# Two semaphore waits on TensorE for each block's gathers in a graph attention kernel

## The chip, the cores and the metric

The kernel runs on one core of a Trainium2 chip. The metric is the device time of one execution in microseconds (us). The engines of the core have their own instruction queues: TensorE (PE in the profile, its weight loads PEld), VectorE (DVE), ScalarE (ACT), GpSimd (POOL) and SyncE (SP), which here only issues DMAs.

## What is computed

One layer of attention over the edges of a graph with 12,500 nodes of 128 features (8 heads of 16) and 212,500 edges, sorted by their target node `dst`:

```
h = relu(layernorm(x))
q, v = h @ Wq.T + bq, h @ Wv.T + bv            # per node
k = edge_attr @ Wk.T + bk                      # per edge
in_m, out_m, diag_m = sum(q[src]*k), sum(q[dst]*k), sum(q[src]*q[dst])   # per edge and head
score = (softmax over each dst of in_m + of out_m + of diag_m) * edge_weight**lam
out = x + leaky_relu(segment_sum(score * v[dst]) @ Wo.T + bo, 0.1)
```

The three softmaxes are each taken over the edges of one target node.

## The kernel before

All of the work is in `ordered_path`; a second path, `general_path`, is in the program for other inputs and does not run.

**Preparation** (to about 178 us in the profile). Node features are loaded and normalized, q is computed and written to a table in device memory (`q_table`), once more as three bf16 terms (`q3_table`). Indices of the edges are brought into shape. On the way, the first gathers and edge loads are issued.

**The edge loop** (line 1091) is written out in full. Edges come in blocks of 512 (`BE`), 4 to a partition (`JN`). The 416 blocks are cut into S = 5 streams; turn g = 5t + s works on block t of stream s, and there are 420 turns. For each turn:

- `gather` (L604): four indirect DMAs on POOL (L608) fetch the rows q[src] into a tile `qq`. They are issued LOOK = 9 turns ahead; `qq` has QQ = 11 buffers, so the gathers of block b wait until DVE has read block b - 11.
- `fetch_edges` (L593): SP loads the edge features, 6 turns ahead.
- `turn` (L937): PE transposes the edge features, ACT copies them out of PSUM (L942).
- `project` (L946): PE makes k: one matmul for the bias (L948) and four f32 matmuls, 8 instructions in the profile (L950). `k_ps` has two PSUM buffers, so k of block g waits for DVE's multiply of block g - 2.
- `spread_q` (L955): PE multiplies the one-hot rows `oh` by a window of the q table (L959) to get q[dst], since targets are sorted; ACT copies it to `qq` (L961). ACT makes the one-hots from the relative targets in two operations (L934, L935, `one_hots`).
- `logits` (L963): DVE multiplies q[src] by q[dst] (L968), both by k (L969), and sums over each head (L971).

Every fifth turn the logits of five blocks are transposed and scanned on DVE along the edges: a running maximum (L1001, L1004), then running sums of the exponentials (L1025, L1029). The sums at the ends of segments are picked by a one-hot matrix (`select`, L1038; PE, L1062) and written to device memory.

**The last part** (from about 2300 us) divides the sums, multiplies by v, applies Wo and writes the output.

The order of each engine's instructions is the order in which the program calls them: `pin` (L575) ties each instruction to the one before it on its engine, by an order without a semaphore, and keeps the name of the last one in `pinned[engine]`. In turn g the calls come in this order: `gather(g + 9)`, `fetch_edges(g + 6)`, `project(g + 1)`, `turn(g + 2)`, `spread_q(g + 2)`, `logits(g)`, `one_hots`, and then the work of the scans, which differs with s. So k of block g is made by PE at the start of turn g - 1.

Blocks 0 to 8 are gathered in the preparation code (L868), the others in the loop; POOL has nothing else to do in the loop.

Of the kernel before, what the change touches and what calls it, by code (L numbers as in the profile page):

```python
# [472 lines left out]
def ordered_path(ctx: ExitStack, tc: tile.TileContext, flag, x, src, dst, edge_attr, edge_weight,  # L473
# [17 lines left out]
    nc = tc.nc  # L491
# [76 lines left out]
    LOOK, QQ, AHEAD, EA = 9, 11, 6, 7  # L568
# [4 lines left out]
    pinned = {}  # L573

    def pin(inst):  # L575

        engine = str(inst.ins.engine)
        if engine in pinned:
            tc.add_manual_dep(inst.ins, pinned[engine], mybir.DependencyInfo(
                mybir.DependencyClass.NoSync, mybir.DependencyReason.DATA), reason="in order")  # L580
        pinned[engine] = inst.ins.name
        return inst
# [5 lines left out]
        q.dma_start(to[cut:RW - 1, :], t[cut * RC:top].rearrange("(r c) -> r c", c=RC))  # L588
        q.dma_start(to[RW - 1:RW, :E - top], t[None, top:E])

    qqs, st, eas = {}, {}, {}

    def fetch_edges(g):  # L593
        if g < S * T:
            ea = load.tile([P, JN * F], F32, name="ea", bufs=EA)
            b0 = (g % S * G + g // S) * BE
            n = min(BE, E - b0)
            if n < BE:
                nc.vector.memset(ea, 0.0)
            pin(nc.sync.dma_start(ea[:n // JN, :],  # L600
                                  edge_attr[b0:b0 + n, :].rearrange("(p j) f -> p (j f)", j=JN)))
            eas[g] = ea

    def gather(g):  # L604
        if g < S * T:
            qq = gath.tile([P, JN, 2, F], F32, name="qq")
            for j in range(JN):
                pin(nc.gpsimd.indirect_dma_start(  # L608
                    out=qq[:, j, 0, :], out_offset=None, in_=q_table,
                    in_offset=bass.IndirectOffsetOnAxis(  # L610
                        ap=src_i[:, g % S * G + g // S, j:j + 1], axis=0)))
            qqs[g] = qq

    def units(t, lo, n, c):
# [13 lines left out]
    with tc.tile_pool(name="prep", bufs=1) as prep, \  # L628
# [239 lines left out]
        for g in range(LOOK):  # L868
            gather(g)
# [30 lines left out]
    with tc.tile_pool(name="work", bufs=2) as work, \  # L900
# [5 lines left out]
        def block_rows(t):  # L906
            lo = t if t < G else t - 1
            return lo, slice(0, S * G) if t < G else slice(1, S * G + 1)

        def fetch(t):  # L910

            if t >= T:
                return
            at, part = block_rows(t)
            relb = load.tile([K3, S, BE], BF, name="relb")
            pin(nc.sync.dma_start(relb, rel_d[part].rearrange("(s b) e -> s b e", b=G)
                                  [None, :, at, :].to_broadcast([K3, S, BE])))
            fa = load.tile([4 * S, BE], BF, name="fa", bufs=4)
            for s in range(S):
                pin(nc.sync.dma_start(fa[4 * s:4 * s + 4], fa_d[s * G + t]))  # L920
            _, base_v[t] = nc.values_load_multi_w_load_instructions(
                bases[0:1, t, 0:S], engines=[mybir.EngineType.SP], min_val=0, max_val=N - 1,
                skip_runtime_bounds_check_because="the indices of nodes are below N")
            win = load.tile([K3, S, F], BF, name="win")
            for s in range(S):
                pin(nc.sync.dma_start(win[:, s, :], q3_table[bass.ds(base_v[t][s] * 3, K3), :]))
            st[t] = dict(relb=relb, fa=fa, win=win)

        def one_hots(t, s):

            if s == 0:
                st[t]["oh"] = work.tile([K3, S, BE], BF, name="oh")
            d = st[t]["relb"][:, s, :]
            pin(nc.scalar.activation(d, d, AF.Abs, bias=before[:K3]))  # L934
            pin(nc.scalar.activation(st[t]["oh"][:, s, :], d, AF.Relu, bias=1.0, scale=-1.0))  # L935

        def turn(g):  # L937
            eT_ps = ps.tile([P, JN, P], F32, name="eT_ps", bufs=2)
            for j in range(JN):
                pin(nc.tensor.transpose(eT_ps[:, j, :], eas[g][:, j * F:(j + 1) * F], ident))  # L940
            eT = work.tile([P, JN, P], F32, name="eT", bufs=3)
            pin(nc.scalar.copy(eT, eT_ps))  # L942
            eTs[g] = eT
            del eas[g]

        def project(g):  # L946
            k_ps = ps.tile([P, JN, F], F32, name="k_ps", bufs=2)
            pin(nc.tensor.matmul(k_ps, ones3, bk3, start=True, stop=False))  # L948
            for j in range(JN):
                pin(nc.tensor.matmul(k_ps[:, j, :], eTs[g][:, j, :], wk, start=False,  # L950
                                     stop=(j == JN - 1)))
            ks[g] = k_ps
            del eTs[g]

        def spread_q(g):  # L955
            s, d = g % S, st[g // S]
            qd_ps = ps.tile([P, JN, F], F32, name="qd_ps")
            for j in range(JN):
                pin(nc.tensor.matmul(qd_ps[:, j, :], d["oh"][:, s, j * P:(j + 1) * P],  # L959
                                     d["win"][:, s, :], start=(j == 0), stop=(j == JN - 1)))  # L960
            pin(nc.scalar.copy(qqs[g][:, :, 1, :], qd_ps))  # L961

        def logits(g):  # L963
            s, t = g % S, g // S
            if s == 0:
                lTs[t] = scan.tile([P, JN, S, H3], F32, name="lT")
            prod = work.tile([P, JN, 3, F], F32, name="prod")
            pin(nc.vector.tensor_mul(prod[:, :, 2, :], qqs[g][:, :, 0, :], qqs[g][:, :, 1, :]))  # L968
            pin(nc.vector.tensor_mul(prod[:, :, 0:2, :], qqs[g],  # L969
                                     ks[g][:, :, None, :].to_broadcast([P, JN, 2, F])))  # L970
            pin(nc.vector.tensor_reduce(lTs[t][:, :, s, :],  # L971
                                        prod.rearrange("p j i (h d) -> p j (i h) d", d=DIM), AX.X,
                                        ALU.add))
            del ks[g], qqs[g]
# [103 lines left out]
        def later(f, t):  # L1078
            if 0 <= t < T:
                f(t)  # L1080

        fetch(0)
        fetch(1)
        for s in range(S):
# [6 lines left out]
        for g in range(end + 2 * S):  # L1091
            s, t = g % S, g // S
            if g < end:
                gather(g + LOOK)
                fetch_edges(g + AHEAD)
            if g + 1 < end:
                project(g + 1)
            if g + 2 < end:
                turn(g + 2)
                spread_q(g + 2)  # L1100
            if g < end:
                logits(g)
            if t + 1 < T:
                one_hots(t + 1, s)
            if s == 0:
                later(turn_logits, t - 1)
                later(turn_sums, t - 2)
            elif s == 1:
                later(scan_max, t - 1)
            elif s == 2:  # L1110
                later(to_rows, t - 2)
                later(powers, t - 1)
            elif s == 3:
                later(scan_sums, t - 1)
                if t + 2 < T:
                    fetch(t + 2)
            else:
                later(select, t - 1)
                later(put_rows, t - 2)

    edges.close()

# [64 lines left out]
@with_exitstack  # L1187
def kernel(ctx: ExitStack, tc: tile.TileContext, x, src, dst, edge_attr,
                              edge_weight, Wq, bq, Wk, bk, Wv, bv, Wo, bo, lam, out):

    nc = tc.nc
    given = (x, src, dst, edge_attr, edge_weight, Wq, bq, Wk, bk, Wv, bv, Wo, bo, lam, out)
    flags = ctx.enter_context(tc.tile_pool(name="flags", bufs=1))
    flag = flags.tile([1, 1], I32, name="flag")
    ordered_path(tc, flag, *given)
    other = nc.values_load(flag[0:1, 0:1], min_val=0, max_val=1)
    with tc.If(other != 0):
        general_path(tc, *given)  # L1200
# [29 lines left out]
```

## Time and profile before

| what | value |
|---|---|
| median of 4 runs | 2479.02 us (2473.14 to 2480.8) |
| profiled execution | 2478.28 us |
| its span in the trace | 2476.5 us |
| granted TensorE clock, mean | 0.806 |
| PE, DVE, ACT, POOL busy in the span | 71%, 86%, 61%, 68% |
| first and last gather of the run (L608) start | 100.4 us, 2293.9 us |
| L608: count, mean | 1680, 989 ns |
| L968, L969, L971: count and mean | 420 each; 683, 1214, 1753 ns |

Busy time is the time in which an engine executes; waits, and what it takes to issue an instruction, are not in it. In the groups of the page, a line ends with the idle time of the engine just ahead of these instructions and with what ended most of it; "issue" means that the profile shows nothing that it waited for. In the timeline each row has its start, its duration, the engine, the line, the operation, and in brackets the idle time before it and its releaser. The chain of work that ended last is followed back from the last instruction of the run. The windows give each engine's busy time and, in brackets, its number of instructions in a stretch of time, then the granted TensorE clock, the share of the DMA engines and the GB/s.

### The profile page before, as it was taken

How to read it: one execution, taken by the hardware profiler on the slowest of the kernel's cores; microseconds unless marked ns; L12 is line 12 of the kernel's file. 1: busy time of each engine (PE TensorE's matmuls, PEld its weight loads, DVE VectorE, ACT ScalarE, POOL GpSimd, SP SyncE). 2: the span in 40 equal slices, each digit the busy share in tenths (PEclk: the TensorE clock that was granted, in tenths of full speed). 3: DMA queues.
4: the chain of work that ended last, by engine and by line, in shares of the span. 5: the costliest groups of instructions: out<-in, count | busy, mean ns of one | idle time of the engine just before them, and what ended most of it. 6: DMA issues, size and time to landing. Idle time of an engine off the chain costs nothing.

```text
span 2476.5 us, 35097 instructions
## 1 busy us (share of the span) xinstructions
PE 1748.3 (71%) x10635; PEld 1411.6 (57%) x10635; DVE 2139.5 (86%) x2178; ACT 1499.1 (61%) x2806; POOL 1694.2 (68%) x1714
## 2 busy tenths in 40 slices
PE   5327777777677777777777777776777777767476
PEld 4215666665565565556556566565565666656355
DVE  6559999999989899898999989988899988999463
ACT  5547766766566556665656666566565665656354
POOL 2557777777777777777777777777777777777000
PEclk9658888878887778887878878788787787788599
DMA  7755455554444544445444444444444445443532
GB/s 223 241 171 158 142 150 143 143 150 129 136 137 131 148 127 137 138 136 144 128 136 136 143 138 128 137 137 136 141 130 136 136 130 150 129 136 88 118 101 76
DMA packets 307123, 345.21 MB, mean 139 GB/s; under 512 B 134531, under 2 KB 225944, under 8 KB 306613
## 3 DMA queue, kind: packets, MB, share of 16 engines
q1 hardware_dynamic: 252474, 229.91, 30.7%
q0 software_dynamic: 54448, 112.96, 17.8%
q8 instruction: 85, 1.39, 0.2%
q14 instruction: 116, 0.95, 0.1%
HBM read 309.91 MB, written 32.76 MB: 138 GB/s over the span
## 4 chain that ended last, share of the span: by engine, by line
DVE 24%; DMA 23%; issue 18%; POOL 13%; PE 12%; ACT 9%; SPq 0%; DVEq 0%; ACTq 0%; POOLq 0%
DMA qq<-q_table,src_i 20%; POOL qq L608 13%; DVE prod L969 8%; DVE prod L968 6%; PE k_ps L950 4%; DVE sum L1029 2%; PE w_ps L1062 2%; DVE u L1001 2%; DVE lT L971 2%; PE eT_ps L940 1%; DMA q_table<-q 1%; ACT qq L961 1%; ACT relb L934 1%; ACT xq L790 1%; PE o_ps L1173 1%
## 5 line engine op out<-in xcount | busy, mean ns | idle before, releaser
L608 POOL DMA_INDIRECT qq<-q_table,src_i x1680 | 1661.3, 989 | 544.0 <-issue 422.9
L950 PEld LDWEIGHTS k_ps<-wk,eT 128*128 128x128 f32 x3360 | 517.4, 235 | 616.9 <-issue 372.4
L971 DVE TENSOR_REDUCE lT<-prod 128x96 f32<-128x1536 f32 x420 | 736.2, 1753 | 14.3
L942 ACT COPY eT<-eT_ps 128x512 f32<-128x512 f32 x420 | 245.9, 586 | 716.3 <-PE eT_ps L940 714.8
L950 PE MATMUL k_ps<-wk,eT 128*128 128x128 f32 x3360 | 613.0, 338 | 12.9 <-ACT eT L942 8.7
L969 DVE TENSOR_TENSOR prod<-qq,k_ps 128x1024 f32<-128x1024 f32 x420 | 509.8, 1214 | 2.5 <-PE k_ps L950 2.5
L948 PE MATMUL k_ps<-b,ones 3*128 3x512 bf16 x420 | 183.0, 436 | 451.4 <-DVE prod L969 451.2
L968 DVE TENSOR_TENSOR prod<-qq 128x512 f32<-128x512 f32 x420 | 286.8, 683 | 164.1 <-DMA qq<-q_table,src_i 135.1
L940 PE MATMUL eT_ps<-ident,ea 128*128 128x128 f32 x1680 | 323.1, 327 | 2.9 <-DVE found L881 2.9
L934 ACT ACTIVATE relb<-relb,before 126x512 bf16<-126x512 bf16 x420 | 308.2, 734 | 7.3 <-DMA relb<-rel_d 7.3
L935 ACT ACTIVATE oh<-relb 126x512 bf16<-126x512 bf16 x420 | 264.7, 630 | 13.4
L940 PEld LDWEIGHTS eT_ps<-ident,ea 128*128 128x128 f32 x1680 | 258.7, 174 | 3.2 <-DVE found L881 3.2
L961 ACT COPY qq<-qd_ps 128x512 f32<-128x512 f32 x420 | 248.1, 591 | 0.7 <-PE qd_ps L959 0.7
L959 PE MATMUL qd_ps<-win,oh 126*128 126x128 bf16 x1680 | 199.0, 252 | 36.7 <-ACT oh L935 30.8
L1062 PE MATMUL w_ps<-back,sel 128*126 128x144 f32 x1344 | 202.3, 308 | 1.3 <-ACT back L1050 1.3
L1049 PE MATMUL b_ps<-ident,sum 120*128 120x120 f32 x672 | 141.6, 344 | 82.0 <-ACT l L991 78.5
L1062 PEld LDWEIGHTS w_ps<-back,sel 128*126 128x126 f32 x1344 | 189.1, 207 | 2.0 <-ACT back L1050 2.0
L959 PEld LDWEIGHTS <-oh 126*128 126x128 bf16 x1680 | 160.6, 116 | 49.7 <-ACT oh L935 32.1
L1049 PEld LDWEIGHTS b_ps<-ident,sum 120*128 120x128 f32 x672 | 102.3, 214 | 132.9 <-ACT l L991 97.9
L1050 ACT COPY back<-b_ps 128x480 f32<-128x480 f32 x168 | 97.5, 580 | 45.4 <-PE b_ps L1049 45.4
L1001 DVE TENSOR_TENSOR_SCAN u<-l,u,far_ps 120x512 f32<-120x512 f32 x83 | 105.5, 1271 | 1.4 <-ACT l L991 1.4
L1029 DVE TENSOR_TENSOR_SCAN sum<-keep,sum,e 120x512 f32<-120x512 f32 x83 | 105.9, 1276 | 0.0
(155 smaller groups left out, 1664.8 us busy)
## 6 DMA issues: line engine op xcount, KB each, us to landing
ea<-in_edge_attr_dram SPq DMA_DIRECT2D x419, 256.0 KB
relb<-rel_d SPq DMA_DIRECT2D x84, 630.0 KB
qq<-q_table,src_i POOLq DMA_INDIRECT x1680
win<-q_table SPq DMA_DIRECT2D x420, 31.5 KB
q_table<-q SPq DMA_DIRECT2D x24, 384.0 KB
fa<-fa_d SPq DMA_DIRECT2D x420, 4.0 KB
sums<-rows SPq DMA_DIRECT2D x416, 7.9 KB
q_table<-xq SPq DMA_DIRECT2D x24, 256.0 KB
```

The source lines that it names most:

```text
L608: pin(nc.gpsimd.indirect_dma_start(out=qq[:, j, 0, :], out_offset=None, in_=q_table, in_offset=bass.IndirectOffsetOnAxis(ap=src_i[:, g % S ...
L934: pin(nc.scalar.activation(d, d, AF.Abs, bias=before[:K3]))
L935: pin(nc.scalar.activation(st[t]["oh"][:, s, :], d, AF.Relu, bias=1.0, scale=-1.0))
L940: pin(nc.tensor.transpose(eT_ps[:, j, :], eas[g][:, j * F:(j + 1) * F], ident))
L942: pin(nc.scalar.copy(eT, eT_ps))
L950: pin(nc.tensor.matmul(k_ps[:, j, :], eTs[g][:, j, :], wk, start=False, stop=(j == JN - 1)))
L959: pin(nc.tensor.matmul(qd_ps[:, j, :], d["oh"][:, s, j * P:(j + 1) * P], d["win"][:, s, :], start=(j == 0), stop=(j == JN - 1)))
L961: pin(nc.scalar.copy(qqs[g][:, :, 1, :], qd_ps))
L968: pin(nc.vector.tensor_mul(prod[:, :, 2, :], qqs[g][:, :, 0, :], qqs[g][:, :, 1, :]))
L969: pin(nc.vector.tensor_mul(prod[:, :, 0:2, :], qqs[g], ks[g][:, :, None, :].to_broadcast([P, JN, 2, F])))
L971: pin(nc.vector.tensor_reduce(lTs[t][:, :, s, :], prod.rearrange("p j i (h d) -> p j (i h) d", d=DIM), AX.X, ALU.add))
L1062: pin(nc.tensor.matmul(w_ps[:, i].rearrange("p s c -> p (s c)"), d["sel"][:, j, lo:lo + 3, :].rearrange("p s w -> p (s w)"), d["back"][:, ...
```

## The change

Two of each block's four gathers get a dependency with a semaphore on an instruction of TensorE. `behind[g, 0]` is the last product of k of block g, noted after `project(g)`; `behind[g, 2]` is the last TensorE instruction of turn g - 1, noted at the end of that turn. The gathers of block g + 9 look them up: the first (j = 0) waits for `behind[g, 0]`, the third (j = 2) for `behind[g, 2]`. The second and fourth follow in POOL's queue. The keys begin with g = 1, so blocks 0 to 9 get no such wait. ACT makes the one-hots before and after the change.

```diff
-    qqs, st, eas = {}, {}, {}
+    qqs, st, eas, behind = {}, {}, {}, {}
...
             for j in range(JN):
-                pin(nc.gpsimd.indirect_dma_start(
+                rows = pin(nc.gpsimd.indirect_dma_start(
                     out=qq[:, j, 0, :], out_offset=None, in_=q_table,
                     in_offset=bass.IndirectOffsetOnAxis(
                         ap=src_i[:, g % S * G + g // S, j:j + 1], axis=0)))
+                if (g - LOOK, j) in behind:
+                    tc.add_manual_dep(rows.ins, behind[g - LOOK, j], mybir.DependencyInfo(
+                        mybir.DependencyClass.Sync, mybir.DependencyReason.SCHED_ONLY),
+                        reason="close behind the products")
...
+        products = str(mybir.EngineType.PE)
         fetch(0)
...
             if g + 1 < end:
                 project(g + 1)
+                behind[g + 1, 0] = pinned[products]
...
                 later(put_rows, t - 2)
+            behind[g + 1, 2] = pinned[products]
```

## The prediction

> **What bounds the kernel now.** I read the page first (engine shares, chain, costliest groups), then POOL's own waits, the POOL column of the windows, the chain in order of time, and the timeline at the start of the edge loop.
>
> The page has VectorE (DVE) busy for 86% of the span and POOL for 68%, so DVE looks like the bound. The chain and the group of L608 say otherwise:
>
> ```profile
> DVE 24%; DMA 23%; issue 18%; POOL 13%; PE 12%; ACT 9%; SPq 0%; DVEq 0%; ACTq 0%; POOLq 0%
> ...
> L608 POOL DMA_INDIRECT qq<-q_table,src_i x1680 | 1661.3, 989 | 544.0 <-issue 422.9
> ...
> L968 DVE TENSOR_TENSOR prod<-qq 128x512 f32<-128x512 f32 x420 | 286.8, 683 | 164.1 <-DMA qq<-q_table,src_i 135.1
> ```
>
> A gather costs POOL 989 ns and 0.30 us of "issue" before the next one can begin. In the timeline that gap is 0.30 or 0.31 us ahead of every gather from 184.06 us to the last one at 2293.9 us, whoever is named as its releaser. So 1636 gathers run there without one wait, (2293.9 - 184.06) / 1635 = 1.290 us each, or 5.16 us for a block of four. The windows of POOL's line show the same pace everywhere, 232 to 235 gathers in 300 us:
>
> ```profile
> 184.00:484.00 300.00, 229.50 (x232) 0.86 0.52 147
> 584.00:884.00 300.00, 229.01 (x234) 0.81 0.48 136
> 1084.00:1384.00 300.00, 229.29 (x233) 0.80 0.48 137
> 1584.00:1884.00 300.00, 229.60 (x232) 0.83 0.48 136
> 1984.00:2284.00 300.00, 228.67 (x235) 0.80 0.45 128
> ```
>
> DVE alone would be faster. In the early windows it is 99% busy with 91 instructions in 100 us; five blocks have 21 of its instructions, so it takes 100 / (91/21) / 5 = 4.6 us a block against POOL's 5.16. The prefetched lead lasts only for a while: from a block's last gather to the DVE multiply that reads it (L968) the trace has 38 us for block 11, 22 us for block 45, 9 us for block 70, and from about block 80 (some 545 us) 3.7 to 5 us to the end, which is one gather and its landing. From there the chain in order of time reads like this:
>
> ```profile
> 1193.50 0.95 POOL qq L608
> 1194.45 0.30 issue
> 1194.75 2.36 DMA qq<-q_table,src_i
> ```
>
> The end of the loop is thus the start of POOL's unbroken run, plus 1.29 us for each gather in it, plus a landing and the last blocks. That is the model for everything below.
>
> **The change, part by part.** No instruction of arithmetic and no byte is added or removed. Two semaphore waits a block are added on POOL: the first gather of block g+9 waits for the last product of k of block g, the third for TensorE's last instruction of turn g-1. Behind a waiting gather stand all later gathers on POOL's one queue, and behind these L968.
>
> *Where a wait can bind.* In the steady part the lead is one block, so the gather of block g+9 runs when TensorE is about eight blocks past block g: k of block g had ended 41 to 45 us before that gather at every tenth block I read from 90 on, and TensorE's turn g-1 some 40 us before. There the waits are met long before and cost nothing. They can bind only where POOL is a full nine blocks ahead, at the start. Block 9 has no wait (no key exists yet). Block 10 is the case. Its four gathers now run in the preparation, before 162.3 us; then POOL sleeps until DVE frees the first buffer, and gather 11 starts at 184.06:
>
> ```profile
> 161.20 1.12 POOL L608 DMA_INDIRECT qq<-q_table,src_i  x1 [0.30 <-issue]
> ...
> 182.10 1.22 DVE L969 TENSOR_TENSOR prod<-qq,k_ps 128x1024 f32<-128x1024 f32 x1 [2.49 <-PE k_ps L950]
> 182.53 1.78 PEld L950 LDWEIGHTS k_ps<-wk,eT 128*128 128x128 f32 x8 [0.44 <-issue]
> 182.53 2.08 PE L950 MATMUL k_ps<-wk,eT 128*128 128x128 f32 x8
> 183.36 1.75 DVE L971 TENSOR_REDUCE lT<-prod 128x96 f32<-128x1536 f32 x1
> 184.06 0.94 POOL L608 DMA_INDIRECT qq<-q_table,src_i  x1 [21.74 <-issue]
> ...
> 185.25 0.63 PE L959 MATMUL qd_ps<-win,oh 126*128 126x128 bf16 x4
> ```
>
> The reader sees the price of a bound wait here: L969 ends at 183.32 and the released gather begins at 184.06, 0.74 us later. The PE row of 182.53 is k of block 1. After the change block 10 waits for its end, 182.53 + 2.08 = 184.61, so its first gather begins at 184.61 + 0.74 = 185.35. Its third can begin 0.74 us after the end of turn 0 (185.25 + 0.63 = 185.88), at 186.6, and POOL reaches it only at 185.35 + 2 x 1.29 = 187.9: no wait. Four gathers end the block at 185.35 + 5.16 = 190.51, where block 11 begins instead of at 184.06. **Term 1: +6.45 us.** Of it 1.29 us is waiting; 5.16 us is work that filled idle time in the preparation and now stands in the run that sets the end.
>
> *Does block 11 wait too?* It needs k of block 2, whose eight products end at 187.35, and the end of turn 1 at 188.01; both lie over 2 us before 190.5. Block 12 would begin at 195.7 and needs 189.6, block 13 at 200.8 and needs 191.9. TensorE then moves about 3.5 us a block and later 4.6, POOL 5.16, so the distance grows and no later block waits. **Term 2: 0.**
>
> *What the preparation gains.* Without these four gathers the preparation has four transfers of 64 KB less in its last 25 us; at the 161 GB/s of 160 to 185 us that is 256 KB / 161 GB/s = 1.6 us of all DMA engines. ACT's L821 waits there for stores of q, so up to 1.6 us of the loop's start could come earlier. The other end is 0. I take 0: forty gathers stay where they are, and block 10's landed before the last transfers that the loop waits for (relb, win) were issued. **Term 3: 0, from -1.6.**
>
> *The queue.* The waits need some 840 more instructions of the semaphore kind on POOL's queue. One takes 43 ns where it finds its semaphore met. The existing one of each block ends 7.3 us (median) before the gather that it belongs to, for the queue runs ahead of the engine, and the gap ahead of a block's first gather is no longer than that of the others (0.305 us both). So they are hidden: **term 4: 0**; if that cover were gone, up to 840 x 0.043 = 36 us.
>
> *Collisions with DVE.* A gather takes 0.944 us undisturbed. Of 218 that began within an L968 161 took over 1.0 us, most of them about 1.39; of 405 that began within L969 none did, nor of 541 within L971. L968 has both inputs in SBUF, L969 has one in PSUM. All stretching in the run is 68 us. Until DVE has used up its lead (some 360 us) a stream that is 6 us later meets DVE at other phases: those 360 us hold about 14 us of stretching, which could go to 0, or double. The five windows pass through all phases and differ by 3 gathers in 233, so I take **term 5: 0, within 4 us either way**, which is also the spread of the four runs.
>
> The Trainium skill's page "SBUF — State Buffer", section "Who interferes with whom", says that a VectorE instruction with two SBUF inputs contends with a GpSimd instruction that reads SBUF, and that whichever began first holds the port while the other stands still. The first half fits these rows; the second doesn't, for L968 takes at most 0.76 us though gathers of 0.94 us are often under way. By that rule the change would do well to keep gathers clear of L968, which would be worth all 68 us if its waits bound; by the rows they don't bind.
>
> Sum on the profiled execution: 2478.28 + 6.45 = **2484.7 us**. The median of the runs is 0.7 us above that execution, so I forecast 2485 us, 0.25% slower. A measurement of this kernel can tell about 0.2% (5 us) from no change.
>
> **The rivals.**
>
> *The delay is given back* (not slower): term 3 at its far end and fewer collisions take 3 to 6 us off: 2479 to 2482. For it speak only the bounds of terms 3 and 5; against it, that neither has a reason to go one way. To it belongs that no wait is made at all and the program runs as before: 2479.
>
> *The pairs do keep clear of L968* (faster): if waits bind as long as DVE is the slower one, the first 360 us lose their 14 us of stretching: 2484.7 - 14 = 2471, and more if the phase held on. It decides from the point where k of block g ends after POOL is free for block g+9; the row of block 12 (195.7 against 189.6) speaks against it.
>
> *The waits are paid on the queue* (much slower): the extra semaphore instructions stand in the 0.30 us gap instead of ahead of it: up to 36 us, 2521; a quarter of it 2494.
>
> **How the numbers follow.** Forecast (one bound wait, block 10 moved into the run) 0.72; its own range is 2479 to 2489 (term 3 to -1.6, term 5 within 4), three quarters of it above the 2484.0 that 0.2% means: slower 0.54, same 0.18. Given back or no wait 0.14, all same. Kept clear 0.06, faster. Paid on the queue 0.08, slower. So faster 0.06, same 0.32, slower 0.62. The range 2477 to 2491 holds the first two and leaves out most of the others.
>
> **What would show it.** Right: 40 gathers before POOL's long sleep instead of 44, the next at about 185.3 released by PE, the last near 2300.4 instead of 2293.9, all other gaps 0.30, the mean gather still near 989 ns, the last L968 6 us later. Term 2 is wrong if POOL has gaps over 0.4 us behind 190 us; term 4 if the gap ahead of first and third gathers grows; term 5 if the mean moves by over 3 ns (1640 x 3 ns = 5 us); term 3 if L968 of block 0 begins before 178.9. The forecast falls if POOL's run has waits that recur, or if its last gather begins before 2296.

## The result, and the profile after

The changed kernel takes 2483.48 us (median of 42 runs, 2474.16 to 2493.46); the kernel before took 2478.29 us beside it (63 runs). The ratio is 1.0022 [1.0016, 1.0029]: 5.2 us slower by the medians, against a forecast of 6.45 us. The profiled execution took 2483.24 us with a span of 2481.4 us, 4.9 us more than the span before. The granted TensorE clock was 0.807 (0.806 before).

The lines of the page that answer to those of before, after a shift of four line numbers (L968 is now L972, L950 is L954):

```profile
PE 22%; DVE 20%; DMA 19%; issue 18%; ACT 12%; POOL 7%; DVEq 0%; SPq 0%; ACTq 0%; POOLq 0%
...
L608 POOL DMA_INDIRECT qq<-q_table,src_i x1680 | 1656.6, 986 | 552.6 <-issue 336.2
...
L972 DVE TENSOR_TENSOR prod<-qq 128x512 f32<-128x512 f32 x420 | 286.7, 683 | 166.7 <-DMA qq<-q_table,src_i 128.7
```

Read alone, the chain would tell a story: PE has gone from 12% to 22%, POOL from 13% to 7%, as if gathers now waited for TensorE all along. POOL's own waits say how often they did. Columns: us in total, number of times, longest.

```profile
POOL qq L608 <- issue: 336.2, 1103, 0.3
...
POOL qq L608 <- PE k_ps L954: 48.2, 60, 30.3
```

Of 60 idle times that end at L954, one is 30.3 us long; the other 59 share 48.2 - 30.26 = 17.9 us, 0.30 us each. That is the gap that every gather has, whoever is named for it. So there is one wait, and the timeline around it, ahead of block 10, is this:

```profile
154.41 0.95 POOL L608 DMA_INDIRECT qq<-q_table,src_i  x1 [0.30 <-issue]
...
182.85 1.22 DVE L973 TENSOR_TENSOR prod<-qq,k_ps 128x1024 f32<-128x1024 f32 x1 [2.49 <-PE k_ps L954]
...
183.28 2.07 PE L954 MATMUL k_ps<-wk,eT 128*128 128x128 f32 x8
...
185.62 0.94 POOL L608 DMA_INDIRECT qq<-q_table,src_i  x1 [30.26 <-PE k_ps L954]
...
188.11 0.94 POOL L608 DMA_INDIRECT qq<-q_table,src_i  x1 [0.30 <-PE eT_ps L944]
...
189.36 1.44 POOL L608 DMA_INDIRECT qq<-q_table,src_i  x1 [0.30 <-issue]
...
191.10 0.94 POOL L608 DMA_INDIRECT qq<-q_table,src_i  x1 [0.30 <-DVE prod L973]
```

Forty gathers come before the sleep (the fortieth at 154.41) and the forty-first is released by k of block 1. The third gather of the block (188.11) does not wait. Block 11 begins at 191.10 instead of 184.06, 7.0 us later. The windows of POOL's line show the pace of before, 230 to 235 gathers in 300 us (us, busy and number, clock, DMA share, GB/s):

```profile
184.00:484.00 300.00, 228.56 (x230) 0.84 0.51 146
584.00:884.00 300.00, 228.98 (x234) 0.79 0.48 135
1084.00:1384.00 300.00, 229.59 (x232) 0.80 0.48 136
1584.00:1884.00 300.00, 228.68 (x235) 0.84 0.49 138
1984.00:2284.00 300.00, 228.67 (x235) 0.80 0.46 129
```

And the end of the loop in the timeline, the last gather and the last L972:

```profile
2297.35 0.94 POOL L608 DMA_INDIRECT qq<-q_table,src_i  x1 [0.30 <-issue]
...
2302.03 0.69 DVE L972 TENSOR_TENSOR prod<-qq 128x512 f32<-128x512 f32 x1 [0.33 <-DMA qq<-q_table,src_i]
```

The last gather is 3.5 us later than before. Block 11 began 7.0 us later, so 3.6 us were given back on the way. All of it is the length of single gathers: over the 1636 gathers from block 11 on, the time above 0.944 us each adds up to 64.4 us, against 68.0 us before; the gaps between them add up to 498.4 us against 498.3 us.

### The profile page after: what moved, and what is told of

Read it like the earlier page. It is cut to its first block, busy times and chain, and to the rows that moved or that the text cites. A ratio compares the mean times of both kernels' runs of the same rounds, so it can differ in the third digit from the quotient of the medians.

```text
span 2481.4 us, 35917 instructions
## 1 busy us (share of the span) xinstructions
PE 1745.6 (70%) x10635; PEld 1409.3 (57%) x10635; DVE 2139.5 (86%) x2178; ACT 1500.3 (60%) x2806; POOL 1689.6 (68%) x1714
## 3 DMA queue, kind: packets, MB, share of 16 engines
q0 software_dynamic: 54448, 112.96, 17.9%
q8 instruction: 85, 1.39, 0.2%
## 4 chain that ended last, share of the span: by engine, by line
PE 22%; DVE 20%; DMA 19%; issue 18%; ACT 12%; POOL 7%; DVEq 0%; SPq 0%; ACTq 0%; POOLq 0%
DMA qq<-q_table,src_i 18%; PE k_ps L954 8%; DVE prod L973 7%; POOL qq L608 7%; DVE prod L972 4%; PE w_ps L1066 4%; PE eT_ps L944 3%; DVE sum L1033 2%; PE k_ps L952 2%; ACT relb L938 2%; DVE u L1005 2%; ACT qq L965 2%; ACT l L995 2%; PE b_ps L1053 1%; DVE ew L1029 1%
## 5 line engine op out<-in xcount | busy, mean ns | idle before, releaser
L954 PEld LDWEIGHTS k_ps<-wk,eT 128*128 128x128 f32 x3360 | 516.0, 235 | 623.3 <-issue 365.4
L954 PE MATMUL k_ps<-wk,eT 128*128 128x128 f32 x3360 | 611.3, 338 | 11.6 <-ACT eT L946 7.9
L973 DVE TENSOR_TENSOR prod<-qq,k_ps 128x1024 f32<-128x1024 f32 x420 | 509.9, 1214 | 2.5 <-PE k_ps L954 2.5
L972 DVE TENSOR_TENSOR prod<-qq 128x512 f32<-128x512 f32 x420 | 286.7, 683 | 166.7 <-DMA qq<-q_table,src_i 128.7
L963 PE MATMUL qd_ps<-win,oh 126*128 126x128 bf16 x1680 | 199.3, 252 | 36.4 <-ACT oh L939 30.5
L963 PEld LDWEIGHTS <-oh 126*128 126x128 bf16 x1680 | 160.6, 116 | 49.4 <-ACT oh L939 31.8
```

The costliest lines, as they stand in the source:

```text
L973: pin(nc.vector.tensor_mul(prod[:, :, 0:2, :], qqs[g], ks[g][:, :, None, :].to_broadcast([P, JN, 2, F])))
```

## The experiments

The theory: the end is where POOL's unbroken run starts, plus 1.29 us for each gather in it; the change moves four gathers into the run and adds a short wait. The rivals: its semaphore instructions cost time on POOL's queue; or the later stream meets DVE at other phases and the difference is collisions.

The table gathers what the traces show for the kernels that ran beside a kernel before of 2478 to 2480 us. "Ahead" is the number of gathers before POOL's long sleep; "stretching" is the time above 0.944 us of the gathers from block 11 on; "tail" is from the last gather's start to the end of the span. All but the ratio are of one execution each.

| kernel | ahead | first gather after the sleep | last gather | stretching | tail | ratio |
|---|---|---|---|---|---|---|
| before | 44 | 184.06 | 2293.88 | 68.0 | 182.6 | 1 |
| after | 40 | 185.62 | 2297.35 | 64.4 | 184.1 | 1.0022 [1.0016, 1.0029] |
| e1, waits from block 11 | 44 | 188.08 | 2290.06 | 60.1 | 181.1 | 1.0015 [1.0002, 1.0028] |
| e2, wait of block 10 alone | 40 | 183.60 | 2293.37 | 62.4 | 181.0 | 1.0020 [1.0006, 1.0034] |
| e3, seven turns ahead | 32 | 183.60 | 2306.43 | 65.8 | 183.6 | 1.0054 [1.0037, 1.0072] |
| e9, waits from block 13 | 44 | 189.85 | 2296.25 | 64.5 | 189.9 | 0.9998 [0.9988, 1.0009] |
| e10, ten turns ahead | 48 | 186.08 | 2292.82 | 70.0 | 189.1 | 0.9983 [0.9969, 0.9997] |
| e12, the change again | 40 | 186.13 | 2297.08 | 64.1 | 181.3 | 1.0006 [0.9993, 1.0018] |
| e4, product from PSUM | 44 | 184.83 | 2272.31 | 45.6 | 183.2 | 0.9922 [0.9904, 0.9941] |
| e11, e4 and e10 | 48 | 184.04 | 2271.77 | 50.7 | 185.2 | 0.9916 [0.9901, 0.9932] |

Stretching, tail and the start of the loop each differ by 7 to 10 us between executions of kernels in which DVE has the same work. One trace therefore shows how many gathers stand in the run and whether it has gaps; 5 us of time are decided by the ratios.

**e1: the waits from block 11 on.** The edit of the changed kernel:

```diff
-                if (g - LOOK, j) in behind:
+                if g - LOOK > 1 and (g - LOOK, j) in behind:
```

> All waits of the change stay, but block 10's two are left out (the keys count from g = 2). My theory, that the whole cost is block 10's gathers moved behind TensorE's k of block 1: POOL prefetches 44 gathers again, gather 11 begins near 184 us, the ratio to the kernel before is 1.000 (within 0.0007), although some 818 semaphore instructions more stand in POOL's queue. Rival, that the waits of all blocks are paid on POOL's queue: the ratio stays at 1.002.

It gave 2483.51 us, ratio 1.0015 [1.0002, 1.0028]: not the 1.000 of the theory. In the timeline:

```profile
182.39 1.22 DVE L973 TENSOR_TENSOR prod<-qq,k_ps 128x1024 f32<-128x1024 f32 x1 [2.49 <-PE k_ps L954]
...
186.18 1.16 PE L954 MATMUL k_ps<-wk,eT 128*128 128x128 f32 x8
...
188.08 0.94 POOL L608 DMA_INDIRECT qq<-q_table,src_i  x1 [26.79 <-PE qd_ps L963]
```

Forty-four gathers are ahead, as expected, but now block 11 waits. Its buffer is free at 182.39 + 1.22 = 183.61, which would let it begin 0.74 us later, at 184.35. Its new wait is for k of block 2, which ends at 186.18 + 1.16 = 187.34, and it begins 0.74 us after that: 3.7 us late, 0.15%. (The releaser named, L963, is a later neighbour in the records; POOL's queue passes the wait at 187.38.) This was in the trace of before, 187.35 against 184.06; I had checked block 11 only behind a delayed block 10. So e1 was no test of the queue. Its other gaps are 0.305 us.

**e2: only block 10 waits.**

```diff
-                if (g - LOOK, j) in behind:
+                if g - LOOK == 1 and (g - LOOK, j) in behind:
```

> Only block 10 gets its two waits, no other block does. My theory: ratio 1.002 to 1.003 (5 to 6.5 us), the whole of the change's cost; 40 gathers ahead of POOL's long sleep and the 41st released by TensorE near 185.4 us. Rival, that the waits of all blocks are paid on POOL's queue: 1.000 to 1.0005.

It gave 2484.82 us, 1.0020 [1.0006, 1.0034], the whole slowdown, with two extra semaphore instructions instead of 820. One block's wait is enough to make it. The forty-first gather:

```profile
183.60 0.94 POOL L608 DMA_INDIRECT qq<-q_table,src_i  x1 [28.82 <-PE k_ps L954]
```

It is released by TensorE as expected, but at 183.60 and not near 185.4, since the first multiply of this execution began at 177.64 (178.92 before).

**e3: the same cause, larger.** The kernel before, with gathers seven turns ahead and no wait on TensorE:

```diff
-    LOOK, QQ, AHEAD, EA = 9, 11, 6, 7
+    LOOK, QQ, AHEAD, EA = 7, 8, 6, 7
```

> The kernel before, with no wait on TensorE at all, but with LOOK 7 and 8 buffers of qq in place of 9 and 11: blocks 8, 9 and 10 can't be gathered in the preparation. My theory prices a block that is moved from POOL's idle time into its unbroken run at 5.16 us: 3 x 5.16 = 15.5 us, ratio 1.0062, the last gather near 2309. Rival, that the cost came from the semaphores: 1.000, since DVE has 20 us and more of lead to spare at the start and the steady lead is one block only.

It gave 2491.97 us, 1.0054 [1.0037, 1.0072], which holds the expected 1.0062. The timeline has 32 gathers ahead of the sleep:

```profile
145.67 0.94 POOL L608 DMA_INDIRECT qq<-q_table,src_i  x1 [0.30 <-issue]
183.60 0.94 POOL L608 DMA_INDIRECT qq<-q_table,src_i  x1 [36.99 <-issue]
```

The loop starts no later than before, and three blocks that moved into the run cost 12.0 us by the medians. A shorter prefetch acts like the change, without any semaphore.

**e4: no collisions at L968.** The kernel before, with q[dst] read from PSUM:

```diff
-            eT_ps = ps.tile([P, JN, P], F32, name="eT_ps", bufs=2)
+            eT_ps = ps.tile([P, JN, P], F32, name="eT_ps")
...
-            qd_ps = ps.tile([P, JN, F], F32, name="qd_ps")
+            qd_ps = qds[g] = ps.tile([P, JN, F], F32, name="qd_ps", bufs=2)
...
-            pin(nc.vector.tensor_mul(prod[:, :, 2, :], qqs[g][:, :, 0, :], qqs[g][:, :, 1, :]))
+            pin(nc.vector.tensor_mul(prod[:, :, 2, :], qqs[g][:, :, 0, :], qds.pop(g)))
```

> The kernel before, with DVE's first multiply (L968) reading q[dst] from PSUM in place of its copy in SBUF, so that it has one SBUF input only; qd_ps gets two buffers, eT_ps one. If gathers are stretched because L968 has two SBUF inputs, the some 60 us of stretching that L968 causes go: the mean gather falls from 986 to about 950 ns, POOL's run is 1636 x 1.255 = 2053 us long in place of 2110, and the time is near 2421 us (ratio 0.977). Rival, that it is the start of DVE's work on fresh rows or the writes to prod that stretch a gather: mean still 986 ns, ratio 1.00. Against both: TensorE's next spread now waits for L968, and DVE alone needs some 4.6 us a block, so less than 0.977 can't come of it and TensorE could become late (ratio over 0.985).

It gave 2460.89 us, 0.9922 [0.9904, 0.9941]: faster, but a third of what was expected. Of its page:

```profile
L608 POOL DMA_INDIRECT qq<-q_table,src_i x1680 | 1637.2, 975 | 546.2 <-issue 429.8
```

Counted in the trace, 188 gathers begin within an L968 and none of them takes over 1.0 us. The stretching that L968 caused, 60.2 us before, is gone to 0.0. But the total fell only from 68.0 to 45.6 us, because two other DVE operations with both inputs in SBUF now do it: gathers that begin within L1038 are stretched by 34.7 us in all (6.2 before), within L1004 by 11.5 us (2.2 before). In L1038 they are hardly more, 66 against 64, but they begin 0.26 us into it and not 0.79 us (medians). This is one such meeting in the timeline:

```profile
1212.52 1.02 DVE L1038 TENSOR_TENSOR sel<-ends,places 128x840 f32<-128x840 f32 x1
1212.57 1.79 POOL L608 DMA_INDIRECT qq<-q_table,src_i  x1 [0.30 <-issue]
...
1213.46 0.68 DVE L968 TENSOR_TENSOR prod<-qq,qd_ps 128x512 f32<-128x512 f32 x1
```

The gather that begins 0.05 us into L1038 takes 1.79 us instead of 0.94. The two engines have settled into another phase to each other; why into this one, the runs don't show. The mechanism was right, the size was not: a collision removed at one line came back at another.

**e5 to e8: the same kernels where POOL does not set the pace.** These four ran on another chip, where the kernel before itself took 3391.46 us (15 runs) at a granted clock of 0.70 to 0.71. e5 is the change with waits from block 13 on, e6 is before with ten turns ahead, e7 is e4 and e6 together, e8 the whole change with e4's edit; the edits of the first two are shown at e9 and e10.

> The change with the waits of blocks 10, 11 and 12 left out. In the run with waits from block 11 on, block 11 was held from 184.06 to 188.08 us by k of block 2, which my last expectation overlooked; k of block 3 (189.6 + 0.74 = 190.3) would hold block 12 (189.3) too, k of block 4 (191.9 + 0.74) no longer block 13 (194.3). My theory: gather 11 begins near 184, no gap over 0.31 us behind it, 1.000 (0.9990 to 1.0008), with some 816 more semaphore instructions in the queue. Rival, that a part of the cost is the waits of all other blocks: 1.0015 to 1.002.

> The kernel before, with LOOK 10 and 12 buffers of qq, so that block 11 also is gathered in POOL's idle time (162 to 184 us); room for it comes from edge loads that run 4 turns ahead in 5 buffers in place of 6 in 7. My theory: one block out of POOL's unbroken run is worth 5.16 us, ratio 0.9979, 48 gathers ahead of the long sleep, the last gather near 2289. Rival, that the sleep at the start is covered by DVE's lead: 1.000. If edge loads four turns ahead are too late, TensorE waits for them and the ratio is over 1.

> The kernel with L968 from PSUM and one block more gathered ahead (LOOK 10, 12 buffers of qq, edge loads 4 turns ahead in 5 buffers). If both act on POOL's run alone the gains add: 0.9922 x 0.9979 = 0.990. If DVE or TensorE has become the bound of the L968 version, the block more is worth nothing: 0.992.

> The change as it is (all waits from block 10 on), on the kernel with L968 from PSUM. There one gather takes 0.972 + 0.305 = 1.277 us, so block 10 costs 1.3 us of waiting and 5.1 us of gathers: 6.4 us more than that kernel, ratio to the kernel before 0.9922 + 0.0026 = 0.9948. Rival, that in a kernel with fewer collisions POOL runs far enough ahead for the waits to bind again and again: many gaps of POOL released by TensorE and a ratio over 0.998.

| kernel | median | ratio |
|---|---|---|
| e5, waits from block 13 | 2981.74 us | 0.8799 [0.8786, 0.8813] |
| e6, ten turns ahead | 3387.04 us | 0.9988 [0.9979, 0.9997] |
| e7, product from PSUM, ten ahead | 3195.06 us | 0.9430 [0.9406, 0.9454] |
| e8, the change, product from PSUM | 2956.32 us | 0.8710 [0.8694, 0.8725] |

Only e6's ratio is as expected, and that is luck: its last gather begins at 3144.67 us, not near 2289. The model doesn't hold there, as POOL's waits in e6 show:

```profile
POOL qq L608 <- ACT qq L961: 807.2, 81, 10.5
POOL qq L608 <- issue: 485.2, 1526, 14.9
```

About every fifth turn POOL sleeps for 10 us. The windows of its line have 172 and 169 gathers in 300 us, where the kernel before has 232 and 234 in its trace:

```profile
184.00:484.00 300.00, 172.54 (x172) 0.70 0.37 99
584.00:884.00 300.00, 170.29 (x169) 0.72 0.35 96
```

From block 90 on the last gather of a block in e6 begins 56 to 88 us ahead of the multiply that reads it (median 74), against 4.6 us in the trace of before. POOL's sleeps come 36.5 us apart (median), five turns of 7.3 us, so the lead is 8 to 12 turns, up to all of the 12 buffers, and other work sets the pace: from the first matmul of `w_ps` (L1062) to ACT's copy of the result 17.7 us pass (median), against 2.2 us in the trace of before. In e5, with waits, the lead is 50 us (median), these stretches take 6 us, and the kernel is 12% faster. Single DVE, ACT and POOL instructions last as long as on the other chips (in e6 680 ns for L968 and 947 ns for an undisturbed gather, the same as in e10); TensorE's don't (L950 365 ns in e6, 338 ns in the trace of before). What lengthens these stretches, and why holding gathers back shortens them, the runs don't settle. That part stays open, and these four say nothing about the 0.22%.

**e9: waits from block 13 on, again.**

```diff
-                if (g - LOOK, j) in behind:
+                if g - LOOK > 3 and (g - LOOK, j) in behind:
```

> The waits from block 13 on again, since on the chip of the last set the kernel before itself took 3391 us, 911 more than in the first set, so that the model of POOL's unbroken run doesn't hold there. Where the kernel before takes about 2480 us, my theory says: gather 11 begins near 184 us, no gap of POOL over 0.31 us behind it, ratio 1.000 (0.9990 to 1.0008). Rival, that all waits together cost something on the queue: 1.0015 to 1.002.

It gave 2478.26 us, 0.9998 [0.9988, 1.0009]. Of the change's semaphore instructions 814 are still there, and no cost of theirs is seen: the gaps of the run add up to 498.4 us, to the tenth what they are in the changed kernel, and within 0.1 us of before. In this execution the preparation ended late (its first L972 at 184.71 against 178.92), so gather 45 comes late too, and waits for DVE as before, not for PE:

```profile
187.89 1.22 DVE L973 TENSOR_TENSOR prod<-qq,k_ps 128x1024 f32<-128x1024 f32 x1 [2.49 <-PE k_ps L954]
...
189.85 0.94 POOL L608 DMA_INDIRECT qq<-q_table,src_i  x1 [22.94 <-issue]
```

It begins 0.74 us after L973's end. This was the run to separate the queue from the start. It does so by its trace, where the gaps are those of before, and by an interval that lies below the 1.0016 to 1.0029 of the first set; beside the change itself in its own set (e12 below) the ratio alone doesn't.

**e10: one block more ahead.** The kernel before, with the opposite of the change's effect:

```diff
-    LOOK, QQ, AHEAD, EA = 9, 11, 6, 7
+    LOOK, QQ, AHEAD, EA = 10, 12, 4, 5
```

> LOOK 10, 12 buffers of qq, edge loads 4 turns ahead in 5 buffers, again. Where the kernel before takes about 2480 us: 48 gathers ahead of the long sleep, the last gather near 2289 us, one block out of POOL's unbroken run, ratio 0.9979. Rival, that the sleep at the start is covered by DVE's lead, or that edge loads come too late: 1.000 or more.

It gave 2473.47 us, 0.9983 [0.9969, 0.9997], 5.1 us faster by the medians. Forty-eight gathers are ahead of the sleep:

```profile
168.37 0.94 POOL L608 DMA_INDIRECT qq<-q_table,src_i  x1 [0.30 <-issue]
186.08 0.95 POOL L608 DMA_INDIRECT qq<-q_table,src_i  x1 [16.77 <-issue]
```

Its edit also shortens the lead of the edge loads, from 6 turns to 4, for room; the waits show one for an edge load, of 10.7 us in the preparation, where before has one of 10.9 us. From 32 to 48 gathers ahead the ratio falls by 0.0071, that is 17.6 us / 16 = 1.1 us a gather, where the model has 1.29.

**e11: e4 and e10 together,** the best version that the runs point to.

> L968 from PSUM and one block more gathered ahead, again. Where the kernel before takes about 2480 us: the gains add if POOL's run is still the bound, 0.9922 x 0.9979 = 0.990; 0.992 if DVE or TensorE has become the bound.

It gave 2459.91 us, 0.9916 [0.9901, 0.9932]: faster than both kernels. It isn't shown to be better than e4 alone, whose interval overlaps, and its profiled execution has 50.7 us of stretching against e4's 45.6.

**e12: the change itself, in this set.**

> The change itself, on the same chip as the three others. Where the kernel before takes about 2480 us: 1.0022, by 0.0022 over the version with waits from block 13 on. Where it takes some 900 us longer, the versions with waits were the fast ones (2982 against 3391 us), and this one should be near 0.88 too.

It gave 2482.13 us, 1.0006 [0.9993, 1.0018], with medians 3.6 us apart. Its trace is the one of the changed kernel over again:

```profile
154.45 0.97 POOL L608 DMA_INDIRECT qq<-q_table,src_i  x1 [0.30 <-issue]
186.13 0.94 POOL L608 DMA_INDIRECT qq<-q_table,src_i  x1 [30.71 <-PE k_ps L954]
```

The interval only touches that of the 42 runs (1.0016 to 1.0018 is in both), holds 1, and overlaps that of e9: the expected 0.0022 between the two was 0.0008 by the ratios and isn't shown in this set. Weighting the two measurements of the change by their widths gives 1.0019, 4.6 us: the slowdown is there, and lies at the small end of what the first set says.

## Why the prediction was right

**The bound** was read rightly: of 1639 gaps behind the sleep none is over 0.33 us, nor of the 1635 before. e3 and e10 move the end both ways through the number of gathers ahead, without a wait on TensorE; both also change the number of buffers, and e10 the lead of the edge loads.

**Term 1** (+6.45 us) is right in kind, a little large in size: 5.2 us by the medians of the 42 runs, 4.8 in e2, 4.0 a block in e3, 5.1 in e10, 3.6 in e12. One part is its 0.74 us from the releaser's end to the gather, read off a gather that DVE releases. Behind k of block 1 it was 0.27 us in the changed kernel (185.62 after 183.28 + 2.07 = 185.35), and as much in e2 and e12; behind k of block 2 in e1 it was 0.74. POOL's queue passes the wait 0.06 us after the product's end in the changed kernel (185.41) and 0.04 us after it in e1 (187.38), so the difference lies between the queue and the gather, and what makes it stays open. The rest of the difference is within what stretching and tail vary.

**Term 2** (0, no later wait) held: block 10's is the only one. e1 shows how near it was; with block 10 left early, block 11 waits 3.7 us, against the 6.45 of term 1, and the ratios of e1 and of the change (1.0015, 1.0022) are not told apart. The forecast of a slowdown didn't hang on block 10 alone, which I hadn't seen.

**Term 3** (0, from -1.6) can't be read: the first multiply of block 0 began between 177.64 and 184.71 us in these executions, and at 179.67 in the changed kernel's against 178.92 before. The sign that the forecast gave for it, a first L968 ahead of 178.9, was too fine for one trace. So was the sign that the forecast falls if the last gather begins before 2296: in e2, which has the same slowdown by its ratio, it begins at 2293.37.

**Term 4** (0, up to 36) was 0: 820 more semaphore instructions, 0.1 us of gaps. The cover named was that the queue runs 7.3 us ahead of the engine. e9 keeps nearly all of these instructions, with the same gaps and a ratio of 1 within its interval. The bound for a lost cover was too large: each of the 820 takes 17 ns in the trace of the changed kernel, not the 43 ns of the existing ones, so all of them are 14 us and not 36.

**Term 5** (0, within 4 us) was -3.6 us between the two profiled executions and is inside its bound, in part by luck: over the runs with DVE's code unchanged, stretching went from 60.1 to 70.0 us, more than 4 us either way. This is why the last gather came at 2297.35 and not at 2300.4.

**The rivals.** Given back: 3.6 us were, in one execution, but the ratio shows the slowdown. Kept clear of L968: no, 151 of 217 gathers that began within L972 took over 1.0 us, 161 of 218 before. (The forecast put most of these 161 at about 1.39 us; they go from 1.0 to 1.48, the median is 1.33.) Paid on the queue: no, by the gaps, which are 498.4 us in the changed kernel and in e9 and 498.3 before.

The Trainium skill's page "SBUF — State Buffer", section "Who interferes with whom", was weighed there. e4 bears out its first half with 60.2 us that went to 0.0 when one input moved to PSUM. On its second half, that whichever began first holds the port while the other stands still, the forecast misread the rows. Where DVE began first, the gather stands still: in the trace of before 222 gathers begin within a DVE instruction and take over 1.0 us, and all of them end 0.81 to 0.83 us after that instruction's end. Where the gather begins with L968, L968 is the longer one: 11 of 420 take over 0.70 us, and each has a gather that begins between 0.02 us ahead of it and 0.04 us into it and keeps its 0.94 us, as here:

```profile
807.16 0.76 DVE L968 TENSOR_TENSOR prod<-qq 128x512 f32<-128x512 f32 x1
807.20 0.94 POOL L608 DMA_INDIRECT qq<-q_table,src_i  x1 [0.30 <-issue]
```

An L968 that begins later within a gather takes at most 0.70 us. So a gather delays DVE only around its own start, by up to 0.08 us, and L968's small maximum, which the forecast held against the page, is no sign against its rule; but no row shows a gather that holds DVE up for the whole of its 0.94 us.

## What to carry to other kernels

Where one queue runs without a break to the end, a wait that binds once at its start costs not only the wait but all the prefetched work that it moves out of idle time into the run. Before adding a wait, set the time at which its releaser ends against the time at which the instruction could go, row by row for every block that still runs ahead, and once more for the next block with the first left alone. An engine's share of the chain was no measure of waiting here: read the number and the longest of its waits.

## What the hardware showed beyond that

An f32 operation of DVE with both inputs in SBUF (L968, L1004, L1038) lengthens an indirect gather that begins within it, except within its first 0.04 us: the gather then ends some 0.82 us after the operation. That makes of 944 ns up to 1.48 us with an L968 of 683 ns and 1.79 us with an L1038 of 1.02 us, and almost nothing for a gather that begins near the operation's end. An operation with an input in PSUM doesn't do it, not even a longer one (L969, 1.21 us). On another chip the same program took 3391 us instead of 2479, with equal times of single DVE, ACT and POOL instructions and a clock of 0.71 instead of 0.81, and there the waits of the change from block 13 on were worth 12%: a pace set by one engine on one chip need not be the bound on the next.
